# Fixing TensorE's order in the attention of a gated cross-attention and mixture-of-experts block

## The chip, the core and the metric

The kernel runs on one core of a Trainium2 chip. The metric is the device time of one execution in microseconds (us), as the median over several executions. One of them is also taken with the hardware profiler, whose rows the text quotes. PE is TensorE, DVE VectorE, ACT ScalarE, POOL GpSimd, SP SyncE.

## The reference

The input `x` holds 4 x 1024 tokens of 256 values. Each batch entry has 64 context tokens. What is computed, in float32 throughout:

```python
def attention(q, k, v):                       # 16 heads of 64
    qh, kh, vh = q @ w_qs, k @ w_ks, v @ w_vs # per head
    attn = softmax(qh @ kh.T)
    out = (attn @ vh) * qh                    # times the queries
    return concat_heads(out) @ w_proj.T + b_proj

def experts(x):                               # 8 experts, 256 -> 1024 -> 256
    w, sel = top_k(x @ gate_w.T, 2)
    combine = scatter(softmax(w), sel)
    return sum_e(combine[:, e] * (silu(x @ w1[e]) @ w2[e]))

x = x + tanh(g_xattn) * attention(layernorm(x), ctx, ctx)
x = x + tanh(g_ffn) * experts(layernorm(x))
```

## The kernel before

The 4096 tokens are cut into `NG` = 8 groups of 512, and each group into `T` = 4 tiles of 128, which are the steps of the main loop (L1330 to L1378). Two groups belong to one batch entry (`GB` = 2). Sixteen heads are handled as `NP` = 8 pairs. The loop runs over `g` from 0 to 8 and, in it, over `t` from 0 to 3. It is a software pipeline. In step `t` of group `g` stand:

- `probabilities` (L424 to L443): the scores `sc` of the tile in a PSUM pool of two, 16 records on PE, then on DVE the maximum `mx` and the difference `pr`, on ACT the exponential, on DVE the sum `sm` and its reciprocal, and on POOL the product `pr` with the reciprocal.
- `transpose_probabilities` (L454): eight transposes `pa` of the previous step's probabilities, copied by ACT into `aT`. In the program these follow the scores directly.
- `attend` (L469), at step 1 for the previous group: probabilities by values, `po`, in two halves of four head pairs; DVE multiplies each with the queries in `qT` (L478).
- `queries` (L408): the next group's queries, 512 columns for each pair, `pq`, over the steps as `parts` says: four pairs, two, one and one.
- `project` (L486), at steps 2 and 3 for the previous group: `pp`, 32 records of 256 columns for two tiles, which DVE adds to the residual `x` (L493).
- For each pair of groups whose attention is done, the functions `after` and `placing` prepare the experts in eight steps: batch statistics (step 0), the second layernorm's tiles (L312) and their transposes `pt_b` (L317) with the logits `pl` (L508), turned over by a transpose `pl_t` (L518) for the pair's first group (step 1) and the second (step 2), the routing `route` on DVE (step 3), and then `placing` (step 4): the products `prow` (L565, L566) count the tokens ahead of each one. From step 4 on POOL writes the tokens into a table by indirect DMA (L606).
- `ln_norm(g + 2, …)`, at step 2's end: the tiles `xn_a` (L312) of the first layernorm, their transposes `pt_a`, and ACT's copies of them. The tiles live in a pool of three buffers.

`route` compares all logits (L531 to L534), ranks them, and derives `chosen`, a running count `prior`/`taken` of eight pairs of small instructions (L543, L544), and the two weights (L547 to L556). Its `cmp` and `placing`'s `of_choice` share a pool of two buffers with the probabilities `pr`.

The experts run in slots: nine early ones of 256 tokens taken from the first half of the tokens, then wide ones over the rest. A slot's pieces (`ph`, `hT`, `py`) are given out by a generator, `slots`. In groups 6, 7 and the pass after them (`pieces`), some early pieces are handed to the end of a step, as a filling between attention's products; the rest follow after the loop.

What the order of the work comes from: the kernel lists instructions in program order, and a scheduler orders those of each engine by priority and by their estimated costs, unless an instruction is pinned by `pinned(instruction, True)`, which keeps it in program order among the pinned ones. Before the change hardly any of attention's PE instructions is pinned. The scheduler therefore puts `pl` and `pt_a` between scores and moves halves of `po` and products around them. PSUM has a rotating pool of four banks for all products but the scores.

Of the kernel before, what the change touches and what calls it, by code (L numbers as in the profile page):

```python
# [21 lines left out]
def kernel(  # L22
# [254 lines left out]
    def pinned(instruction, pin=True):  # L277
        if pin:
            tc.keep_in_program_order(instruction)

    def ln_stats(groups, name):
        n = len(groups) * T
        mv = small.tile([P, n, 2], F32, tag="mv", name=f"mv_{name}")
        for i in range(n):
            st = small.tile([P, 6], F32, tag="st", name=f"st_{name}_{i}")
            first = nc.vector.bn_stats(st, xg[groups[i // T]][:, i % T, :])
            pinned(first, name == "a0" or i == 0 and name[0] == "a")
            pinned(nc.vector.bn_aggr(mv[:, i, :], st), name == "a0")
        rstd = small.tile([P, n, 1], F32, tag="rstd", name=f"rstd_{name}")
        if name[0] == "a":  # L290
            pinned(nc.scalar.activation(rstd, mv[:, :, 1:2], AF.Sqrt, bias=eps), name == "a0")
            pinned(nc.vector.reciprocal(rstd, rstd), name == "a0")
        else:
            nc.vector.tensor_scalar(rstd, mv[:, :, 1:2], EPS, None, ALU.add)
            nc.gpsimd.tensor_tensor(rstd, rstd, power.unsqueeze(2).to_broadcast([P, n, 1]), ALU.pow)
        return {g: (mv[:, k * T : (k + 1) * T], rstd[:, k * T : (k + 1) * T]) for k, g in enumerate(groups)}

    def ln_norm(g, stats, name):

        mv, rstd = stats[g]  # L300
        nT[g] = npool.tile([P, NC, G], F32, tag="nT", name=f"nT_{name}_{g}")
        first = g == 0 and name == "a"
        keep = None
        if name == "b":
            keep = xg[g]
        elif first:
            keep = npool.tile([P, T, D], F32, tag="nT", name=f"keep_{name}_{g}")
        pt = [bank(f"pt_{name}_{g}_{c}", first) for c in range(NC)]
        for t in range(T):
            xn = keep[:, t, :] if keep is not None else work.tile([P, D], F32, tag="xn", name=f"xn_{name}_{g}_{t}")  # L310
            with behind_sums() if name == "b" else nullcontext():
                scale = nc.vector.tensor_scalar(  # L312
                    xn, xg[g][:, t, :], mv[:, t, 0:1], rstd[:, t, :], ALU.subtract, ALU.mult
                )
            pinned(scale, first)
            for c in range(NC):
                turn = nc.tensor.transpose(  # L317
                    pt[c][:, t * P : (t + 1) * P], xn[:, c * P : (c + 1) * P], ident
                )
                pinned(turn, first)  # L320
        for c in range(NC):
            copy = nc.vector.tensor_copy if first and c else nc.scalar.copy
            pinned(copy(nT[g][:, c, :], pt[c]), first)
# [47 lines left out]
    def values(ctxT):  # L371

        n = 512 // P
        for b0 in range(0, B, 2):
            for p0 in range(0, NP, n):
                pv = bank(f"pv_{b0}_{p0}")
                for c in range(NC):
                    nc.tensor.matmul(
                        pv,
                        ctxT[:, c, b0 * M : (b0 + 2) * M],  # L380
                        wv[:, c, p0 * P : (p0 + n) * P],
                        start=(c == 0),
                        stop=(c == NC - 1),
                    )
                pvv = pv.rearrange("p (q j r k) -> p q j r k", j=2, r=2, k=DK)
                q0 = p0 // 2
                for i in range(2):
                    to = vs[:, b0 + i].rearrange("p (q r) k -> p q r k", r=2)
                    for j in range(2):
                        nc.scalar.copy(  # L390
                            to[j * M : (j + 1) * M, q0 : q0 + n // 2],
                            pvv[i * M : (i + 1) * M, :, j],
                        )
                yield
# [9 lines left out]
    def queries(g, qT, pairs):  # L404
        for p in pairs:
            pq = bank(f"pq_{g}_{p}")
            for c in range(NC):
# [4 lines left out]
                    start=(c == 0),  # L412
                    stop=(c == NC - 1),
                )
                pinned(product, (g, p, c) == (0, 0, 0))
            nc.scalar.copy(of_pair(qT, p), pq)  # L416

    newest = []
# [1 line left out]
    def probabilities(g, t, qT):  # L420

        sc = ps2.tile([P, NP // 2, 2, 2, M], F32, tag="ps2", name=f"sc_{g}_{t}")
        for p in range(NP):
            nc.tensor.matmul(  # L424
                sc[:, p // 2, :, p % 2, :],
                of_pair(qT, p)[:, t * P : (t + 1) * P],
                kT[g // GB][:, p, :],
# [20 lines left out]
    def transpose_probabilities(g, t, pr, aT):  # L448
        prv = pr.rearrange("p (i j) m -> p i (j m)", j=2)
        n = 512 // P  # L450
        for p0 in range(0, NP, n):
            pt = bank(f"pa_{g}_{t}_{p0}")
            for i in range(n):
                nc.tensor.transpose(pt[:, i * P : (i + 1) * P], prv[:, p0 + i, :], ident)  # L454
            nc.scalar.copy(  # L455
                aT[p0 // n][:, :, t * P : (t + 1) * P], pt.rearrange("p (i q) -> p i q", i=n)
            )
# [1 line left out]
    def attend(g, pairs, qT, aT):  # L459

        for q in range(pairs[0] // 2, pairs[-1] // 2 + 1):
# [3 lines left out]
            for r in range(2):  # L465
                for j in range(2):
                    half = slice(j * M, (j + 1) * M)
                    i = q * 2 + r
                    nc.tensor.matmul(  # L469
                        po[j][r * DK : (r + 1) * DK],  # L470
                        vs[half, g // GB, i, :],
                        of_pair(aT, i)[half],
# [7 lines left out]
    def project(g, qT, t0):  # L480

        pp = bank(f"pp_{g}_{t0}").rearrange("p (t d) -> p t d", d=D)
        for i in range(2):
            t = t0 + i
            for p in range(NP):
                nc.tensor.matmul(  # L486
                    pp[:, i, :],
                    of_pair(qT, p)[:, t * P : (t + 1) * P],
                    wp[:, p, :],
# [13 lines left out]
    def logits(g, lg):  # L503

        pl = bank(f"pl_{g}")[:, :P]
        for c in range(NC):
            for t in range(T):
                nc.tensor.matmul(  # L508
                    pl[t * W : (t + 1) * W],
                    gw[:, c, :],  # L510
                    nT[g][:, c, t * P : (t + 1) * P],
# [2 lines left out]
                )  # L514
        lT = work.tile([P, D], F32, tag="xn", name=f"lT_{g}")[:, :P]
        nc.vector.tensor_copy(lT, pl)
        pt = bank(f"pl_t_{g}")[:, :P]
        nc.tensor.transpose(pt, lT, ident)  # L518
        first = g % GB * T
        nc.vector.tensor_copy(  # L520
            lg[:, first : first + T], pt.rearrange("p (t w) -> p t w", w=W)[:, :, :E]
        )

    def route(lg, name):

# [35 lines left out]
    def place(groups, routing, name):  # L561

        rank, weight, chosen, prior = routing
        pr = bank(f"prow_{name}")[:, : R * E]
        nc.tensor.matmul(pr, earlier, chosen.rearrange("p t e -> p (t e)"), start=True, stop=False)  # L565
        nc.tensor.matmul(pr, ones, prior.rearrange("p t e -> p (t e)"), start=False, stop=True)  # L566
        row = scores_of([R, E], f"row_{name}")
        nc.vector.tensor_tensor(
            row,
# [47 lines left out]
    def counts(name):  # L617

        pn = bank(f"pn_{name}")[:, :E]
        nc.tensor.matmul(pn, ones, taken, start=True, stop=True)  # L620
        count = const.tile([1, E], F32, tag=f"count_{name}", name=f"count_{name}")
        nc.vector.tensor_copy(count, pn[0:1, :])
        return count
# [636 lines left out]

    held = {}

    def finish(g, step):

        qT, aT = held[g]
        if step == 1:
            attend(g, range(NP // 2, NP), qT, aT)
        elif step >= 2:
            project(g, qT, (step - 2) * 2)

    def leave(g):
        apart("out", nc.scalar.dma_start(of[g], xg[g]), f"out{g // HG}")

    second = {}
    entered = 0
    done = in_use = None

    def after(g, step):
# [4 lines left out]
            second.update(ln_stats(groups, f"b{g}"))  # L1283
        elif step == 1:
            second["logits"] = scores_of([R, E], f"lg_{g}")
            ln_norm(groups[0], second, "b")
            logits(groups[0], second["logits"])
        elif step == 2:
            for h in groups[1:]:
                ln_norm(h, second, "b")  # L1290
                logits(h, second["logits"])
        elif step == 3:
            second["routing"] = route(second["logits"], f"{g}")
        if step >= 4:
# [8 lines left out]
    def placing(g):  # L1303
# [17 lines left out]
        {1: ([0, 1, 2], [3, 4], [5, 6], [7]), 2: ([], [], [], [0, 1])},  # L1321
        {2: ([2, 3, 4], [5], [6], [7])},
    ]
    parts += [{g + 1: ([0, 1, 2, 3], [4, 5], [6], [7])} for g in range(2, NG - 1)] + [{}, {}]
    value_parts = (2, 1, 1, 0)
    qTs = [halves("qT_0")]
    queries(0, qTs[0], range(NP - 2))
    ln_norm(1, stats, "a")
    queries(0, qTs[0], range(NP - 2, NP))
    for g in range(NG + 1):  # L1330
        attention_ends = g == NG
        if g < NG:
            qT, aT = qTs[g], halves(f"aT_{g}", "hidden" if g % 2 and g + 1 < NG else "group")
            held[g] = (qT, aT)
# [3 lines left out]
        for t in range(T):  # L1338
            if t == 0 and g >= 2:
                leave(g - 2)  # L1340
            if g < NG:
                pr = probabilities(g, t, qT)
            if last:
                transpose_probabilities(*last)

            b = (g - GB - 1) // GB
            ends, behind = b * GB + GB - 1, (g - GB - 1) % GB * T + t if b >= 0 else -1
            if behind == T:
                placing(ends)
            if g and t == 1:  # L1350
                attend(g - 1, range(NP // 2), *held[g - 1])
            for h, pairs in parts[g].items():
                queries(h, qTs[h], pairs[t])
            if 0 <= g - 1 < NG:
                finish(g - 1, t)
            last = (g, t, pr, aT) if g < NG else None
            if g == 0:
                for _ in range(value_parts[t]):
                    next(pending_values)
            if behind >= 0:  # L1360
                after(ends, behind)
            if g == 0 and t == 1:
                tc.keep_in_program_order(nc.scalar.activation(tg, tg, AF.Tanh))
                tc.keep_in_program_order(
# [1 line left out]
                )  # L1366
                for h in range(2):
                    add_bias(h)
            if g + 2 < NG:
                if t == 0 and (g + 2) % GB == 0:  # L1370
                    stats = ln_stats(list(range(g + 2, g + 2 + GB)), f"a{g + 2}")
                elif t == 2:
                    ln_norm(g + 2, stats, "a")
                    add_bias(g + 2)
            if g < 2:
                clear(g * T + t, 2 * T)
            for _ in range(pieces[g][t] if g in pieces else 0):
                next(slots)  # L1378

    leave(NG - 1)  # L1380
    for step in range(2 * T):
        if step == T:
            placing(NG - 1)
        after(NG - 1, step)
        for _ in range((1, 1, 1, 2, 1, 1, 1, 1)[step]):
            next(slots)
    for _ in slots:
# [44 lines left out]
```

## Time and profile before

| | us |
|---|---|
| median of 3 runs | 878.94 (878.19 to 879.98) |
| profiled execution | 880.53 |
| its span | 878.7 |
| PE busy | 842.2 |
| DVE busy | 496.0 |
| ACT busy | 244.6 |
| POOL busy | 265.9 |
| mean granted PE clock (share of full) | 0.987 |

The span is the time from the first to the last instruction of the profiled execution. The busy times of the engines lie beside each other, so they add up to more than the span. A matmul's end in the profile is modelled; two records that run one behind the other are shown overlapping, and the distance between their starts is what PE needs for one.

The first scores of each group start at 65.6 (group 1), 106.6, 150.9, 200.4, 245.6, 295.05 and 340.35 us (group 7); the last projection begins at 435.70, and the first wide slot's products at 539.9.

### The profile page before, as it was taken

What the parts mean: (1) busy time and instruction counts of PE and PEld (TensorE: products, weight loads), DVE (VectorE), ACT (ScalarE), POOL (GpSimd) and SP (SyncE); (2) the same over time, 40 slices, a digit from 0 to 9 for tenths busy, and PEclk for the clock granted to TensorE, in tenths of its full rate; (3) what the DMA queues carried; (4) which work ended last, traced back from release to release, by engine and by line L of the source; (5) the groups of instructions that cost most, each with busy time, mean ns of one, the idle gap of its engine ahead of it and who ended that gap; (6) DMA issues with size and microseconds to landing.
All of it is one profiled execution on the core that took longest, in us unless ns stands there. A gap on an engine that the chain in (4) does not pass through costs nothing.

```text
span 878.7 us, 13306 instructions
## 1 busy us (share of the span) xinstructions
PE 842.2 (96%) x4684; PEld 681.6 (78%) x4684; DVE 496.0 (56%) x1202; ACT 244.6 (28%) x413; POOL 265.9 (30%) x216
## 2 busy tenths in 40 slices
PE   8999999999999999999999699999999999999996
PEld 5555858485767768785888489899999999899995
DVE  4466384679557966862138443665556753546520
ACT  2663242334332323440112012222222221222210
POOL 3052212223721373207224532123222232222132
PEclk9999999999999999999999699999999999999998
DMA  9999999201100055426675668686667675546611
GB/s 197 336 340 341 340 346 340 85 1 60 61 25 1 25 174 163 108 68 189 165 203 147 173 147 215 164 237 140 144 165 178 157 218 133 133 115 176 184 22 37
DMA packets 165032, 141.79 MB, mean 161 GB/s; under 512 B 72685, under 2 KB 159076, under 8 KB 161248
## 3 DMA queue, kind: packets, MB, share of 16 engines
q1 hardware_dynamic: 145456, 118.79, 46.5%
q0 software_dynamic: 12912, 17.11, 10.1%
q10 hardware_dynamic: 6592, 4.98, 1.8%
q8 instruction: 39, 0.64, 0.3%
q14 instruction: 33, 0.27, 0.1%
HBM read 78.73 MB, written 62.46 MB: 161 GB/s over the span
## 4 chain that ended last, share of the span: by engine, by line
PE 77%; DVE 12%; issue 4%; POOL 2%; ACT 2%; DMA 1%; SPq 0%; POOLq 0%; DVEq 0%; ACTq 0%
PE py L1183 20%; PE ph L955 14%; PE ph L1005 11%; PE pp L486 9%; PE pq L408 8%; PE q L1073 5%; PE sc L424 4%; PE pa L454 2%; DVE mx L433 2%; PE po L469 2%; DVE sm L440 1%; DVE pr L435 1%; DVE qT L478 1%; POOL table L606 1%; POOL pr L443 1%
## 5 line engine op out<-in xcount | busy, mean ns | idle before, releaser
L1146 POOL DMA_INDIRECT out_dram<-x,ids x69 | 108.7, 1575 | 306.8 <-DVE x L1161 102.0
L1183 PE MATMUL py<-w,hT 128*128 128x256 f32 (+1 forms) x960 | 186.0, 362 | 0.0
L1183 PEld LDWEIGHTS py<-w,hT 128*128 128x128 f32 (+1 forms) x960 | 160.0, 181 | 21.6 <-issue 1.7
L955 PE MATMUL ph<-xT,w 128*128 128x256 f32 x576 | 135.9, 390 | 7.2 <-issue 7.2
L955 PEld LDWEIGHTS ph<-xT,w 128*128 128x128 f32 x576 | 111.0, 196 | 26.7 <-issue 12.0
L443 POOL TENSOR_TENSOR pr<-pr,sm 128x1024 f32<-128x1024 f32 x32 | 61.4, 1918 | 208.4 <-DVE sm L441 143.0
L408 PE MATMUL pq<-nT_a,wq 128*128 128x512 f32 x256 | 116.1, 597 | 5.7 <-DVE qT L478 3.9
L486 PE MATMUL pp<-wp,qT 128*128 128x256 f32 x512 | 113.5, 379 | 1.3 <-issue 1.3
L486 PEld LDWEIGHTS pp<-wp,qT 128*128 128x128 f32 x512 | 97.0, 190 | 20.0 <-issue 7.4
L408 PEld LDWEIGHTS pq<-nT_a,wq 128*128 128x128 f32 x256 | 46.2, 190 | 58.2 <-issue 44.0
L963 ACT ACTIVATE hT<-ph 128x1024 f32<-128x1024 f32 (+1 forms) x40 | 37.2, 940 | 192.7 <-PE ph L955 119.3
L606 POOL DMA_INDIRECT table<-x,to_row x64 | 62.5, 976 | 42.7 <-DVE x L595 24.8
L424 PEld LDWEIGHTS sc<-keys,qT 128*128 128x128 f32 x512 | 62.6, 192 | 11.2 <-issue 10.8
L424 PE MATMUL sc<-keys,qT 128*128 128x128 f32 x512 | 67.1, 278 | 0.0
L1161 DVE TENSOR_SCALAR x<-py,ids 128x256 f32<-128x256 f32 (+1 forms) x53 | 24.8, 468 | 69.8 <-PE py L1183 63.8
L455 ACT COPY aT<-pa 128x512 f32<-128x512 f32 x64 | 34.7, 592 | 84.1 <-PE pa L454 74.0
L433 DVE TENSOR_REDUCE mx<-sc 128x16 f32<-128x1024 f32 x32 | 39.0, 1219 | 28.0 <-PE sc L424 27.9
L440 DVE TENSOR_REDUCE sm<-pr 128x16 f32<-128x1024 f32 x32 | 39.0, 1219 | 23.9 <-ACT pr L438 21.5
L478 DVE TENSOR_TENSOR qT<-po,qT 128x512 f32<-128x512 f32 x64 | 40.9, 679 | 13.7 <-PE po L469 9.7
L1019 ACT ACTIVATE hT<-hT 128x384 f32<-128x384 f32 (+1 forms) x66 | 33.1, 501 | 51.1 <-DVE hT L1016 48.2
L416 ACT COPY qT<-pq 128x512 f32<-128x512 f32 x64 | 36.5, 581 | 35.3 <-PE pq L408 34.5
L1005 PE MATMUL ph<-x,sa 128*128 128x192 f32 (+1 forms) x264 | 43.6, 314 | 2.0 <-issue 2.0
(278 smaller groups left out, 999.9 us busy)
## 6 DMA issues: line engine op xcount, KB each, us to landing
w<-in_L_ffn_w_dram SPq DMA_DIRECT2D x58, 1024.0 KB
table<-empty SPq DMA_DIRECT2D x8, 5016.0 KB
x<-table SPq DMA_DIRECT2D x116, 64.0 KB
out_dram<-x ACTq DMA_DIRECT2D x8, 512.0 KB
x<-in_x_dram SPq DMA_DIRECT2D x7, 512.0 KB
out_dram<-x,ids POOLq DMA_INDIRECT x69
wq<-in_L_xattn_w_qs_dram SPq DMA_DIRECT2D x4, 256.0 KB
wv<-in_L_xattn_w_vs_dram SPq DMA_DIRECT2D x2, 512.0 KB
```

The source lines that it names most:

```text
L408: product = nc.tensor.matmul(pq, wq[:, c, p * P : (p + 1) * P], nT[g][:, c, :], start=(c == 0), stop=(c == NC - 1),)
L424: nc.tensor.matmul(sc[:, p // 2, :, p % 2, :], of_pair(qT, p)[:, t * P : (t + 1) * P], kT[g // GB][:, p, :], start=True, stop=True,)
L433: nc.vector.tensor_reduce(mx, scv, AX.X, ALU.max)
L440: nc.vector.tensor_reduce(sm, pr, AX.X, ALU.add)
L443: nc.gpsimd.tensor_tensor(pr, pr, sm.unsqueeze(2).to_broadcast([P, H, M]), ALU.mult).ins,
L478: nc.vector.tensor_tensor(own, po[j], own, ALU.mult)
L486: nc.tensor.matmul(pp[:, i, :], of_pair(qT, p)[:, t * P : (t + 1) * P], wp[:, p, :], start=(p == 0), stop=(p == NP - 1),)
L606: nc.gpsimd.indirect_dma_start(out=table.rearrange("r (u w) -> (r u) w", w=2), out_offset=bass.IndirectOffsetOnAxis(ap=to_row[:, k, i : i ...
L955: nc.tensor.matmul(ph[:, i, :], a[:, c, f * P : (f + 1) * P], xT[:, c, :], start=(c == 0), stop=(c == NC - 1),)
L1005: nc.tensor.matmul(to[:, f, :], left[:, (f0 + f) * P : (f0 + f + 1) * P], right, start=not onto and f == 0, stop=True, skip_group_check=on ...
L1146: rows_added = nc.gpsimd.indirect_dma_start(out=outf.rearrange("n (h d) -> (n h) d", d=w)[:rows_of], out_offset=bass.IndirectOffsetOnAxis( ...
L1183: product = nc.tensor.matmul(py[t][i * m : (i + 1) * m], hT[f // per_tile][:, f % per_tile, t * P : t * P + m], b[:, f, i * w : (i + 1) * ...
```

## The change

All PE instructions of attention (scores, transposes, value products, projection, logits, counting products, and for all groups the queries and the first layernorm's transposes) are pinned to program order, and that order is written anew. In a step it is now: at step 1 the first half of `attend`; the scores; the logits `pl` of a group normalised a step before; `prow` if due; the queries; slot pieces in the last two passes; the projection; the transpose `pl_t` of the logits; at step 3 the first layernorm of group `g + 2` (it stood at step 2); the transposes `pa` of the previous step's probabilities; the other parts of `after`; and at step 1 the second half of `attend`. Group 2's queries get the same division over the steps as the others', and the four value products of the start are spread evenly. The logits are a generator now, with its products in a first part and the turning and the copy to `lg` in a second.

```diff
+    steady = False
+    def multiply(*args, **kwargs):
+        pinned(nc.tensor.matmul(*args, **kwargs), steady)
+    def turn(*args):
+        pinned(nc.tensor.transpose(*args), steady)
...
-                pinned(turn, first)
+                pinned(turned, first or steady)
...
-                pinned(product, (g, p, c) == (0, 0, 0))
+                pinned(product, steady or (g, p, c) == (0, 0, 0))
...
         nc.vector.tensor_copy(lT, pl)
+        yield
         pt = bank(f"pl_t_{g}")[:, :P]
-        nc.tensor.transpose(pt, lT, ident)
+        turn(pt, lT, ident)
...
+        yield
...
+    def attend_half(g, half):
+        attend(g, range(half * NP // 2, (half + 1) * NP // 2), *held[g])
...
+    to_route = []
+    def logits_part():
+        for part in to_route:
+            next(part)
...
-            ln_norm(groups[0], second, "b")
-            logits(groups[0], second["logits"])
-        elif step == 2:
-            for h in groups[1:]:
-                ln_norm(h, second, "b")
-                logits(h, second["logits"])
+        if step in (1, 2):
+            ln_norm(groups[step - 1], second, "b")
+            to_route.append(logits(groups[step - 1], second["logits"]))
...
+    parts = [{g + 1: ([0, 1, 2, 3], [4, 5], [6], [7])} for g in range(2)]
...
-    value_parts = (2, 1, 1, 0)
+    value_parts = (1, 1, 1, 1)
...
+        steady = g <= NG
...
+            if g and t == 1:
+                attend_half(g - 1, 0)
             if g < NG:
                 pr = probabilities(g, t, qT)
-            if last:
-                transpose_probabilities(*last)
+            logits_part()
...
-            if g and t == 1:
-                attend(g - 1, range(NP // 2), *held[g - 1])
             for h, pairs in parts[g].items():
-                queries(h, qTs[h], pairs[t])
-            if 0 <= g - 1 < NG:
-                finish(g - 1, t)
-            last = (g, t, pr, aT) if g < NG else None
+                if pairs[t]:
+                    queries(h, qTs[h], pairs[t])
+            for _ in range(pieces[g][t] if g in (NG - 1, NG) else 0):
+                next(slots)
+            if g and t >= 2:
+                project(g - 1, held[g - 1][0], (t - 2) * 2)
...
-            if behind >= 0:
+            logits_part()
+            to_route.clear()
+            if 1 <= behind <= 2 and t == 2:
                 after(ends, behind)
+            if g + 2 < NG and t == 3:
+                ln_norm(g + 2, stats, "a")
+                add_bias(g + 2)
+            if last:
+                transpose_probabilities(*last)
+            last = (g, t, pr, aT) if g < NG else None
+            if behind >= 0 and not (1 <= behind <= 2 and t == 2):
+                after(ends, behind)
+            if g and t == 1:
+                attend_half(g - 1, 1)
...
-            if g + 2 < NG:
-                if t == 0 and (g + 2) % GB == 0:
-                    stats = ln_stats(list(range(g + 2, g + 2 + GB)), f"a{g + 2}")
-                elif t == 2:
-                    ln_norm(g + 2, stats, "a")
-                    add_bias(g + 2)
+            if g + 2 < NG and t == 0 and (g + 2) % GB == 0:
+                stats = ln_stats(list(range(g + 2, g + 2 + GB)), f"a{g + 2}")
...
-            for _ in range(pieces[g][t] if g in pieces else 0):
+            for _ in range(pieces[g][t] if g == HG + 2 else 0):
                 next(slots)
```

After the loop, the two parts of the logits are drawn in the same step.

More of the change, by code (lines that the diff above doesn't have):

```diff
@@ L316, in ln_norm @@
             for c in range(NC):
-                turn = nc.tensor.transpose(
+                turned = nc.tensor.transpose(
                     pt[c][:, t * P : (t + 1) * P], xn[:, c * P : (c + 1) * P], ident
                 )
-                pinned(turn, first)
+                pinned(turned, first or steady)
         for c in range(NC):
@@ L377, in values @@
                 for c in range(NC):
-                    nc.tensor.matmul(
+                    multiply(
                         pv,
@@ L423, in probabilities @@
         for p in range(NP):
-            nc.tensor.matmul(
+            multiply(
                 sc[:, p // 2, :, p % 2, :],
@@ L453, in transpose_probabilities @@
             for i in range(n):
-                nc.tensor.transpose(pt[:, i * P : (i + 1) * P], prv[:, p0 + i, :], ident)
+                turn(pt[:, i * P : (i + 1) * P], prv[:, p0 + i, :], ident)
             nc.scalar.copy(
@@ L468, in attend @@
                     i = q * 2 + r
-                    nc.tensor.matmul(
+                    multiply(
                         po[j][r * DK : (r + 1) * DK],
@@ L485, in project @@
             for p in range(NP):
-                nc.tensor.matmul(
+                multiply(
                     pp[:, i, :],
@@ L507, in logits @@
             for t in range(T):
-                nc.tensor.matmul(
+                multiply(
                     pl[t * W : (t + 1) * W],
@@ L564, in place @@
         pr = bank(f"prow_{name}")[:, : R * E]
-        nc.tensor.matmul(pr, earlier, chosen.rearrange("p t e -> p (t e)"), start=True, stop=False)
-        nc.tensor.matmul(pr, ones, prior.rearrange("p t e -> p (t e)"), start=False, stop=True)
+        multiply(pr, earlier, chosen.rearrange("p t e -> p (t e)"), start=True, stop=False)
+        multiply(pr, ones, prior.rearrange("p t e -> p (t e)"), start=False, stop=True)
         row = scores_of([R, E], f"row_{name}")
@@ L619, in counts @@
         pn = bank(f"pn_{name}")[:, :E]
-        nc.tensor.matmul(pn, ones, taken, start=True, stop=True)
+        multiply(pn, ones, taken, start=True, stop=True)
         count = const.tile([1, E], F32, tag=f"count_{name}", name=f"count_{name}")
@@ L1261 @@
     held = {}
[L1263 to L1269, printed above, removed]
+    def attend_half(g, half):
+        attend(g, range(half * NP // 2, (half + 1) * NP // 2), *held[g])
     def leave(g):
@@ L1384 @@
         after(NG - 1, step)
+        for _ in range(2):
+            logits_part()
+        to_route.clear()
         for _ in range((1, 1, 1, 2, 1, 1, 1, 1)[step]):
```

## The prediction

> **What bounds the kernel now.** I read the page first: its busy shares, its slices and its chain.
>
> ```profile
> span 878.7 us, 13306 instructions
> PE 842.2 (96%) x4684; PEld 681.6 (78%) x4684; DVE 496.0 (56%) x1202; ACT 244.6 (28%) x413; POOL 265.9 (30%) x216
> PE   8999999999999999999999699999999999999996
> PEclk9999999999999999999999699999999999999998
> PE 77%; DVE 12%; issue 4%; POOL 2%; ACT 2%; DMA 1%; SPq 0%; POOLq 0%; DVEq 0%; ACTq 0%
> ```
>
> PE is busy for 842.2 of 878.7 us, at full clock in all slices but one. The change adds and removes no product. So it can gain only PE's gaps, and any wait that it puts on PE lengthens the run directly. What stops PE is in the list of PE's waits:
>
> ```profile
> PE pq L408 <- DVE qT L478: 3.9, 5, 1.4
> PE po L469 <- DVE qT L478: 2.6, 2, 1.7
> PE pa L454 <- POOL pr L443: 2.1, 2, 1.3
> PE pt_b L317 <- DVE qT L478: 2.0, 4, 0.7
> PE prow L566 <- DVE prior L543: 0.7, 1, 0.7
> ```
>
> These are small, but a matmul's modelled end hides part of a wait. I therefore took from the PE timeline the usual distance of two starts without a wait: 0.43 us for a 512-column record (pq), 0.216 for 256 columns (pp: 32 records from 193.50 to 200.40), 0.112 in sc, 0.109 in a transpose. What a stretch takes beyond its records times these is its excess. From 48 to 425 us, where attention runs, the excess is 32.4 us. Some 10 of it is no matter of order: 7.5 falls in 400 to 424, where POOL issues table writes back to back and PE advances at their pace, and 2.6 is scattered. The other 22.2 lies where the change works: first halves of po waiting (0.6 to 1.7 in each of eight groups, about 9), second halves 3, logits put between scores 0.6 in each of six groups, 4, pt_b 2, group 7's po 4. That is the most that a new order can win.
>
> Then I followed the longest dependence that the change touches, from the logits to the routing's product prow. PE first, then DVE:
>
> ```profile
> 189.41 0.27 PE L518 MATMUL pl_t<-ident,lT 128*128 128x128 f32 x1
> 193.50 7.07 PE L486 MATMUL pp<-wp,qT 128*128 128x256 f32 x32
> 200.40 1.95 PE L424 MATMUL sc<-keys,qT 128*128 128x128 f32 x16
> 203.06 0.33 PE L565 MATMUL prow<-chosen,earlier 128*128 128x64 f32 x2
> ```
> ```profile
> 189.72 0.19 DVE L520 COPY lg<-pl_t 128x32 f32<-128x32 f32 x1
> 190.47 1.22 DVE L433 TENSOR_REDUCE mx<-sc 128x16 f32<-128x1024 f32 x1
> 192.93 0.68 DVE L531 TENSOR_TENSOR cmp<-lg 128x512 f32<-128x512 f32 x1
> 194.14 1.22 DVE L440 TENSOR_REDUCE sm<-pr 128x16 f32<-128x1024 f32 x1
> 202.25 0.17 DVE L543 COPY prior<-taken 128x8 f32<-128x8 f32 x1
> 202.54 0.75 DVE L493 SCALAR_TENSOR_TENSOR x<-pp,tg,x 128x512 f32<-128x512 f32 x1
> ```
>
> From the end of the logits' copy (189.91) to the end of the last prior (202.42) DVE needs 12.5 us, softmax work of the same step between. PE has a product pair of queries and 6.9 us of pp to do meanwhile and reaches prow at 203.06, 0.6 after its input: the wait is just covered.
>
> **The change, part by part.** PE now issues its attention products as written. X is the end of the step's projection, S that of its scores.
>
> 1. *prow in groups 4 and 6.* pl_t moves behind the projection; prow stands right after the next group's first scores. Ready: pl_t to the copy's end 0.5 (189.41 to 189.91), plus 12.5: X+13.0. PE until then: pl_t 0.1, the moved transposes pt_a 8 x 0.109 with a wait of 1.05 (part 4), pa 0.87, sc 1.79: X+4.7. The queries, projection and transposes behind prow can't pass it. Stall 8.3, twice: 16.6, against 0.7 before. Bounds: the last routing, with no softmax beside it, took 8.0 from copy (462.31) to prior (470.3), a stall of 3.8; with one more mx and pr (2.45) ahead on DVE 10.8. I take 12.5, as a softmax runs in both steps.
> 2. *prow after the last attention step.* There 8.0 + 0.5, less some 1.6 of expert records that stand ahead of it: 6.9. Bounds 3 and 8.5.
> 3. *pt_b at step 1 (groups 3, 5, 7)* now comes after pa, ahead of po's second half. Its four normalised tiles follow the softmax on DVE: scores' end to the reciprocal's is S+5.3 in the timeline (mx 1.2, pr 1.2, exp on ACT 1.06, sm 1.2, handovers), then
>
> ```profile
> 168.57 2.73 DVE L312 TENSOR_SCALAR x<-x,mv_b,rstd_b 128x256 f32<-128x256 f32 x4
> ```
>
> so S+8.2. PE has two query pairs (2 x 1.72), pa 0.87 and pt_b's own 0.87 for cover, to S+5.2. Some 3.3 twice; in group 7 about 4.8, as the exp there stands behind an activation table load (1.28 at 351.54). 11.4, and 1.3 for the last pair. Bounds 4 and 15: without POOL's product beside it those four tiles take 1.39 (446.57).
> 4. *pt_a at step 3 behind the projection.* Its fourth tile needs a buffer that the first tile's transposes free, and DVE takes x<-pp (0.75) first. PE has 0.75 of work until then; the wait is 0.65 in three groups, 1.05 in two with a routing chain beside, 1.3 in the first: 5.4, against nothing to speak of before. Bounds 2 and 9.
> 5. *po.* The first half follows pa with nothing between, so the wait for ACT's aT copies (0.54 each) less PE's cover is about 0.6 in eight groups, 4.8. Second halves, at the step's end, 0.15 each, 0.9, and twice 2.0 where batch statistics or of_choice on DVE hold the po products back (groups 2 and 4). 9.7, bounds 5 and 15.
> 6. *Group 7, step 0.* The slot pieces are now inside the step; ACT has the exp until S+3.9, then a table load 1.28, hT 1.09, a load 1.28 and the aT copies 1.08 (rows 346.10 to 351.54), with handovers of 0.8: S+9.4. PE is there at S+4.3: 5.1, bounds 2 and 7.
>
> The even spread of value products, of the second group's query pairs and the later statistics only reorder work before 100 us, where PE has products queued: nothing, at most 2 if that cover fails. DMAs: the late table's entries follow the same routing. It lies 5.6 us earlier against the last projection and 6.9 us of expert products move ahead of that, so the first wide slot stays covered.
>
> Sum: 16.6 + 6.9 + 11.4 + 1.3 + 5.4 + 9.7 + 5.1 = 56.4 of new excess in place of 22.2: +34.2.
>
> 7. *Clock.* PE's clock drops after PE has stood still, in this trace:
>
> ```profile
> 404.00:408.00 4.00, 1.91 (x8) 0.39 (x8) 1.38 (x2) 0.00 (x0) 3.09 (x4) 0.99 1.14 303
> 408.00:411.00 3.00, 3.00 (x11) 1.56 (x6) 0.69 (x1) 0.00 (x0) 2.39 (x3) 0.50 0.80 164
> 490.00:495.00 5.00, 1.76 (x3) 0.86 (x3) 0.93 (x6) 0.00 (x0) 3.78 (x5) 0.50 0.54 210
> 500.00:502.00 2.00, 2.00 (x6) 1.61 (x5) 1.98 (x14) 0.00 (x0) 1.40 (x1) 0.50 0.95 288
> ```
>
> (Columns: stretch, length, busy time of PE, PEld, DVE, ACT, POOL, granted clock, DMA share, GB/s.) Work resumed at 0.50; 21 records near 498 took 7.45 us instead of 4.54, so a drop costs up to 2.9. I charge the two stalls of 8.3: 5.8, between none and five (also the three of about 5), 14.5. "TensorE: Matmul & The Clock Gate" of the Trainium skill, Part 1, says that the gate halves the clock after one idle window of about 3.4 us and opens after about as long of work; the half clock from 407.9 to 411.3 agrees. Speaking against this change, it would put all five stalls at half clock, an estimate of 1.7 each, 8.5 together, and the time at 921.5.
>
> 34.2 + 5.8 = 40.0 on the profiled execution, 878.7 of span and 880.5 with what lies around it. That is 1.6 over the median of the runs, so 878.9 + 40.0 = 918.9.
>
> **The rivals.**
>
> *The stalls are much shorter: 896.* With DVE's scheduler putting routing ahead of softmax, the chain is the 8.0 of the last routing, and 2 x 4.5 goes; x_b at 1.39 takes off 1.3 three times, part 5's two special waits (4.0) vanish, and no clock drops (5.8): 9.0 + 3.9 + 4.0 + 5.8 = 22.7 less, 896. For it: the softmax result isn't due for a while. Against: its reduce comes ahead by the rows above. Chance 0.24.
>
> *Faster: 877 or less.* The one mechanism is that DVE has the routing ready by X+4.7 and the normalised tiles by S+5.2; then only 56.4 less parts 1 to 3 (36.2), 20.2, stands against 22.2 before: 2 gained, 877, and 12 gained, 867, should half of the 20.2 be covered too. It decides from a chain under 4.7, where rows show 8.0 at best. Chance 0.06, and 0.02 for a draw within 0.2%, about what a measurement of this kernel can tell from no change.
>
> *More follows: 937.* The late routing delays the table's writes so that the first wide slot (539.9) waits for its tokens. About 97 us of expert work lies between it and the last projection, so the cover is wide, but the POOL bursts that cost 12.2 at 480 to 498 could hit another stage. 919 + 12 and, with a second one, + 24: 931 to 943. Chance 0.08. The forecast keeps 0.60.
>
> **How the numbers follow.** The forecast's own range is 905 to 932 (parts 1 to 6 with half of their bounds, clock 0 to 14.5). Taking in the half stalls leaves out about 0.1 on either side (the faster cases below, most of the last rival above): 892 to 934. Slower by over 0.2% has 0.60 + 0.24 + 0.08 = 0.92.
>
> **What would show it.** The waits of PE should list prow <- DVE prior near 24 us in three places, and pt_b <- DVE x near 12; PE's busy share falls to about 92%, with clock slices below 9 near 200, 300 and 440. Wrong would be a prow without a wait: then pl_t's lateness was covered, and the rest of the sum is small.

## The result and the profile after

The changed kernel takes 933.16 us (median of 6 runs, 931.06 to 935.64) against 878.96 for the kernel before measured beside it: a ratio of 1.0618, 95% interval 1.0600 to 1.0637, 54.2 us slower. Its profiled execution, 935.64 us, is the longest of the six and has a span of 933.9. The kernel before took 863 us in some sets of runs and 879 to 881 in others, with the changed kernel moving along, so the experiments below are given as ratios to the kernel before measured beside each.

The head of the changed kernel's page, in the order of the lines shown of before (without the chain, which here is a single write at the end):

```profile
span 933.9 us, 13325 instructions
PE 857.9 (92%) x4684; PEld 688.4 (74%) x4684; DVE 503.0 (54%) x1202; ACT 248.8 (27%) x417; POOL 265.5 (28%) x216
PE   8999999896998689688989979999999999999996
PEclk9999999897999979899899979999999999999998
```

The same 4684 products now fill 92% of a longer span. PE's row drops to 6 or 8 in nine of the slices from the eighth to the twenty-first (the 7 in the twenty-fourth has its like in before's 6), and the clock's row to 7 or 8 in five of them or beside them. PE's longest waits in the changed kernel, without those that the profile gives no releaser for:

```profile
PE prow L285 <- DVE prior L555: 13.0, 3, 6.3
PE pt_b L327 <- DVE x L322: 7.9, 6, 1.5
PE ph L967 <- DVE xT L940: 7.6, 2, 4.0
PE prow L285 <- DVE chosen L552: 7.3, 2, 3.6
PE po L285 <- ACT aT L465: 5.7, 7, 3.9
PE py L1195 <- DVE qT L488: 5.2, 1, 5.2
PE pt_a L327 <- DVE xn_a L322: 4.2, 6, 1.2
```

prow waits 20.3 us in all, where 0.7 stood before. New besides: pt_b at 7.9, pt_a, and ph, the first expert products, which wait for their tokens. The 5.2 of py, at 465 to 470 us, falls where POOL writes the table back to back; the like stretch of the kernel before, between 400 and 424, had 7.5 us beyond its records.

By the starts of a group's first scores (the profiled executions, before and after) the difference is 6.3 us at group 4 (200.40 and 206.69), 20.3 at group 5, 22.8 at group 6 and 34.5 at group 7 (340.35 and 374.88). At the 32 ph records that follow all attention work (486.24 and 542.18) it is 55.9, and the rest of the run is the same. Groups 4 and 6 take 14.0 and 11.8 of it; these are the two with a prow. The largest share, 21.4, arises in group 7 and the pass after it.

The stretch around the first prow, from the timeline of the changed kernel:

```profile
203.79 0.27 PE L289 MATMUL pl_t<-ident,lT 128*128 128x128 f32 x1
203.99 0.75 DVE L503 SCALAR_TENSOR_TENSOR x<-pp,tg,x 128x512 f32<-128x512 f32 x1 [3.83 <-PE pp L285]
204.66 0.18 DVE L531 COPY lg<-pl_t 128x32 f32<-128x32 f32 x1
205.81 1.04 PE L289 MATMUL pa<-ident,pr 128*128 128x128 f32 x8
206.96 1.15 DVE L543 TENSOR_TENSOR cmp<-lg 128x512 f32<-128x512 f32 x1 [1.34 <-PE pa L289]
212.27 0.41 PE L285 MATMUL prow<-chosen,earlier 128*128 128x64 f32 x2 [3.64 <-DVE chosen L552]
216.24 1.84 DVE L555 COPY prior<-taken 128x8 f32<-128x8 f32 x1
218.94 0.69 PE L285 MATMUL prow<-prior,ones 128*128 128x64 f32 x2 [6.26 <-DVE prior L555]
219.42 9.47 PE L418 MATMUL pq<-nT_a,wq 128*128 128x512 f32 x16
229.87 0.22 DVE L590 SCALAR_TENSOR_TENSOR of_choice<-rank,row 128x64 f32<-128x64 f32 x1 [9.90 <-PE pa L289]
```

The logits' copy ends at 204.84, one microsecond after the projection, as DVE takes the projection's result (x, 0.75) first. But the first compare, cmp, begins only at 206.96, and the column in brackets says that DVE idled 1.34 us before it for PE's pa. The scores end near 208.5 and prow's second part starts at 218.94: 10.4 us, in which PE has only the two records of prow's first part. Then the sixteen records of queries take 9.3 us instead of 6.9. The last row is a second wait of the same kind: of_choice, which takes a buffer of the same pool as cmp, waits 9.90 us for pa, which now stands behind the queries. The table's writes follow from it.

### The profile page after: what moved, and what is told of

Read it like the earlier page. It is cut to its first block, busy times and chain, and to the rows that moved or that the text cites. A ratio compares the mean times of both kernels' runs of the same rounds, so it can differ in the third digit from the quotient of the medians.

```text
span 933.9 us, 13325 instructions
## 1 busy us (share of the span) xinstructions
PE 857.9 (92%) x4684; PEld 688.4 (74%) x4684; DVE 503.0 (54%) x1202; ACT 248.8 (27%) x417; POOL 265.5 (28%) x216
## 5 line engine op out<-in xcount | busy, mean ns | idle before, releaser
L1195 PE MATMUL py<-w,hT 128*128 128x256 f32 (+1 forms) x960 | 190.7, 367 | 5.2 <-DVE qT L488 5.2
L1195 PEld LDWEIGHTS py<-w,hT 128*128 128x128 f32 (+1 forms) x960 | 162.7, 184 | 28.6 <-DVE qT L488 6.1
L418 PE MATMUL pq<-nT_a,wq 128*128 128x512 f32 x256 | 121.2, 618 | 1.3 <-DVE qT L488 1.2
L418 PEld LDWEIGHTS pq<-nT_a,wq 128*128 128x128 f32 x256 | 48.3, 199 | 52.4 <-issue 48.3
L285 PEld LDWEIGHTS sc<-keys,qT 128*128 128x128 f32 x512 | 60.5, 194 | 13.9 <-issue 13.9
L285 PE MATMUL sc<-keys,qT 128*128 128x128 f32 x512 | 64.5, 280 | 0.0
```

Of the source, the lines that this page charges most:

```text
L285: pinned(nc.tensor.matmul(*args, **kwargs), steady)
L418: product = nc.tensor.matmul(pq, wq[:, c, p * P : (p + 1) * P], nT[g][:, c, :], start=(c == 0), stop=(c == NC - 1),)
L1195: product = nc.tensor.matmul(py[t][i * m : (i + 1) * m], hT[f // per_tile][:, f % per_tile, t * P : t * P + m], b[:, f, i * w : (i + 1) * ...
```

## The experiments

Each result is a ratio to the kernel before, with its 95% interval. One per cent is 8.8 us at 879, and the differences in us below are worked out with it.

**The changed kernel again.**

> The changed kernel itself once more, beside the kernel before, as the measure for the runs that undo one part of it: the kernel before took 863 here and 879 in its first runs, so ratios and not differences are to be compared. If the change costs the same work in both, 1.062 of before; if part of its cost hung on what made the first runs longer (the stretch in which POOL's table writes hold up the other engines, 11 to 12 us in both first profiles), the ratio stays near 1.06 and that stretch is shorter in both.

1.0616 (1.0598 to 1.0634), with the kernel before at 863.25. The ratio holds. The stretch of table writes at the end of the early slots (from 486 us in the kernel before, from 542 in the changed one) cost 11.4 us over its records in the first profile of the changed kernel and is gone in this one, so it has no part in the difference. What makes it was not tried.

**prow later in its step.**

```diff
-            if behind == T:
-                placing(ends)
             for h, pairs in parts[g].items():
...
             last = (g, t, pr, aT) if g < NG else None
+            if behind == T:
+                placing(ends)
```

> The changed kernel with prow and what hangs on it placed behind the queries and the turned probabilities of its step (groups 4, 6 and the pass after 7) instead of right after the scores. Theory A (prow's place on PE makes the stall): the routing is ready some 15 us after the projection's end by the changed kernel's trace, PE now has 12.4 us of work until then, so the wait at prow falls from 10.4 to about 3 in each of the two groups, and the half clock behind it (2.4 and 3.0 us) goes: some 20 us less, about 913. Theory B (the routing, not prow's place, sets the pace; the table and its readers come when routing ends): group 4 gains its 8 to 10, but in group 6 PE only meets the wait later, at the first expert slot, where ph waits 4.0 us for its tokens now: the tokens' wait grows by about 8, and the gain is about 10, 923.

1.0348 (1.0323 to 1.0373): 23 us of the 54 go with this move alone. PE's waits of this run:

```profile
PE prow L285 <- DVE prior L555: 5.5, 3, 2.4
PE ph L967 <- DVE xT L940: 4.2, 1, 4.2
```

prow's waits fall from 20.3 to 5.5 and the one for tokens in group 7 stays at 4.2. Theory A holds: the products queued behind prow were what paid. The wait for tokens that theory B saw growing did not grow.

**The turned logits ahead of the projection.**

```diff
+            logits_part()
+            to_route.clear()
             if g and t >= 2:
                 project(g - 1, held[g - 1][0], (t - 2) * 2)
...
-            logits_part()
-            to_route.clear()
             if 1 <= behind <= 2 and t == 2:
```

> The changed kernel with pl_t (the turned logits) ahead of the projection again, as in the kernel before, and prow left where the change put it. Theory A (the stall is the routing's length less PE's work between pl_t and prow): the routing starts 6.9 us earlier, the waits at prow fall from 10.4 to about 3.5 in groups 4 and 6, the half clock behind them goes, and the table is written 7 us earlier, so the wait for tokens in group 7 (4.0) goes too: 14 + 5 + 4 = 23 less, about 910. Theory B (other work on DVE, the softmax, takes the 7 us): waits at prow fall by under 3 each, time above 922.

1.0575 (1.0538 to 1.0612), a gain of under 4 us where theory A promised 23. The timeline of this run says why:

```profile
198.11 0.27 PE L289 MATMUL pl_t<-ident,lT 128*128 128x128 f32 x1
198.42 0.19 DVE L531 COPY lg<-pl_t 128x32 f32<-128x32 f32 x1
206.73 1.04 PE L289 MATMUL pa<-ident,pr 128*128 128x128 f32 x8
207.88 1.15 DVE L543 TENSOR_TENSOR cmp<-lg 128x512 f32<-128x512 f32 x1 [1.47 <-PE pa L289]
219.87 0.69 PE L285 MATMUL prow<-prior,ones 128*128 128x64 f32 x2 [6.01 <-DVE prior L555]
```

The logits lie ready from 198.61 on, and cmp still begins at 207.88, right after pa. cmp takes one of two buffers that hold probabilities; the older of these is free only when its probabilities have been turned. The change moved pa from behind the scores to the end of the step, and this is the second thing that holds routing back.

**A buffer for cmp, without and with the early logits.**

```diff
-        cmp = soft.tile([P, 2, R, E, E], F32, tag="pr", name=f"cmp_{name}")
+        cmp = small.tile([P, 2, R, E, E], mybir.dt.uint8, tag="cmp", bufs=1, name=f"cmp_{name}")
```

> The changed kernel with the routing's cmp in a buffer of its own (as 8 bit integers, since the memory is full; its values are 0 and 1) instead of one of the two that hold probabilities. Theory C (formed after the turned logits came early for nothing): routing begins when the turning of the step's probabilities frees cmp's buffer, 2.9 us after the projection, and not when the logits are there, 1.05 after it. Then routing starts 1.9 earlier in groups 4 and 6: 2 to 4 us less in all. Theory A (the logits alone set it): the same within 1.

> Both together: cmp in its own buffer and pl_t ahead of the projection. Theory C: routing can begin 7 us before the projection ends; by the changed kernel's trace it needs about 12 us from the logits' copy, so prow's input is there at most 1 to 3 us after PE reaches prow, in place of 10.4: 15 to 18 less in two groups, 5 less of half clock, 4 less of waiting for tokens in group 7: 22 to 27 less than the changed kernel, about 1.03 of before. If a third thing holds routing (softmax first on DVE), under 8 less.

The buffer alone gives 1.0619 (1.0601 to 1.0637), nothing, as theory A of that run had it: cmp begins at 206.78, half a microsecond after the logits' copy, and one of its four operations then takes 2.36 us beside a POOL addition (x plus bias, 206.95 to 209.93) instead of 0.68, which eats the little that was won. With the logits early as well it is 1.0322 (1.0303 to 1.0340), 26 us less. Each of the two alone is worth nothing or under 4 us, since the other still stands in the way. From the timeline of the run with both:

```profile
196.23 0.69 DVE L543 TENSOR_TENSOR cmp<-lg 128x512 uint8<-128x512 f32 x1
207.78 0.33 PE L285 MATMUL prow<-chosen,earlier 128*128 128x64 f32 x2
208.38 0.43 PE L285 MATMUL prow<-prior,ones 128*128 128x64 f32 x2 [0.26 <-DVE prior L555]
```

Routing now runs beside the projection, and prow follows the scores with a wait of 0.26. One part of the forecast didn't come: of the two waits for tokens the one in the pass after is gone, but the one in group 7 stays, 4.3 us. There of_choice still waits for pa (3.02 us, at 216.72).

**Extra work in the wait.**

```diff
+            if behind == T and g < NG:
+                busy = bank(f"busy_{g}")
+                for _ in range(11):
+                    pinned(nc.tensor.matmul(busy, ident, wq[:, 0, :512], start=True, stop=True))
             if behind == T:
                 placing(ends)
```

> The changed kernel with eleven products of 512 columns, whose result nobody reads, put between the scores and prow in groups 4 and 6: 22 records of 0.43, 9.45 us of PE work where PE stands still for 10.4 now. They add work and take away no wait. Theory (what follows the stall, the queries at half clock, is a cost of standing still): the queries behind prow take 6.9 instead of 9.3 and 9.9, so the kernel gets 5.4 us faster by extra work, 1.055 of before instead of 1.0616. Rival (the queries are slow for another reason, as DVE or ACT being behind): no change, or up to 2 us slower.

1.0580 (1.0548 to 1.0613). The whole time alone doesn't decide, as the interval reaches the changed kernel's. The rows do. Timeline of this run:

```profile
208.54 9.61 PE L1366 MATMUL busy<-wq,ident 128*128 128x512 f32 x22
219.02 0.43 PE L285 MATMUL prow<-prior,ones 128*128 128x64 f32 x2 [0.71 <-DVE prior L555]
219.30 7.08 PE L418 MATMUL pq<-nT_a,wq 128*128 128x512 f32 x16
```

prow's second part comes when it came in the changed kernel, at 219, and the queries behind it take 7.08 instead of 9.47, though nothing changed but that PE had something to do. Windows over the queries' start, in the changed kernel and then in this run (the column after POOL's is the granted clock):

```profile
220.00:224.00 4.00, 4.00 (x6) 1.55 (x5) 0.00 (x0) 0.59 (x1) 0.00 (x0) 0.50 0.00 0
```
```profile
220.00:224.00 4.00, 4.00 (x10) 1.71 (x9) 0.00 (x0) 1.17 (x2) 0.00 (x0) 1.00 0.00 0
```

So 2.4 us in group 4, and 3.0 by the same rows in group 6, are the price of the clock.

**po ahead of the second layernorm.**

```diff
+            if g and t == 1:
+                attend_half(g - 1, 1)
             if behind >= 0 and not (1 <= behind <= 2 and t == 2):
                 after(ends, behind)
-            if g and t == 1:
-                attend_half(g - 1, 1)
```

> The changed kernel with the second half of po ahead of the transposes pt_b at step 1 (groups 3, 5, 7 and the pass after). Theory A (pt_b waits for its tiles because nothing lies between): pt_b's waits, 2.5, 2.0 and 2.5 us beyond its records, fall under 0.7 each, and the slow po and sc records behind it (1.8 and 0.6 in group 3) go with them: 8 to 11 us less, 922 to 925. Rival (DVE is the limit: the po products wait behind the four tiles and the scores' maximum comes later): no more than 3 less, 930 or above.

1.0605 (1.0576 to 1.0634): the rival is right. The wait has another name, and is nearly as long:

```profile
PE pt_b L327 <- DVE qT L488: 6.8, 6, 2.5
```

DVE still has softmax, four tiles and now the po products to do before the short step ends.

**The second layernorm a step later.**

```diff
-            if 1 <= behind <= 2 and t == 2:
-                after(ends, behind)
+            if behind == 2:
+                after(ends, 1)
+                after(ends, 2)
...
-            if behind >= 0 and not (1 <= behind <= 2 and t == 2):
+            if behind >= 0 and behind not in (1, 2):
```

> The changed kernel with the second layernorm's transposes pt_b of both groups behind the projection of step 2 and both groups' logits in step 3. Moving po ahead of pt_b only turned its wait for the tiles into a wait for DVE's po products. Theory A' (pt_b at step 1 is at fault, as whatever stands ahead of it there, DVE has softmax, po products and the four tiles to do in one short step): at step 2 the projection's 6.9 us cover DVE. In groups 3, 5 and 7 step 1 loses 6.4, 3.5 and 6.5 to 7.5 us now beyond its records (waits before and in pt_b 4.0, 3.5 and 5.0, the rest po and scores at half clock behind them), in the waits for tiles and the slow records behind them: 13 to 17 less, 1.042 to 1.047. Rival (DVE's backlog goes on and stops po's second half or the queries there): under 5 less, 1.056 or above.

1.0434 (1.0411 to 1.0457), 16 us less, as theory A' had it. Behind the projection the sixteen transposes are nearly free of waits, and po and scores run at full clock again in group 3:

```profile
170.67 2.02 PE L285 MATMUL po<-aT,vs 64*64 64x512 f32 x16
172.63 2.05 PE L285 MATMUL sc<-keys,qT 128*128 128x128 f32 x16
184.77 0.98 PE L327 MATMUL pt_b<-ident,x 128*128 128x128 f32 x7 [0.49 <-DVE x L503]
```

**The expert pieces at the step's end.** The loop that draws `pieces` in the last two passes goes back behind everything else.

> The changed kernel with the expert pieces of the last two passes at the end of their steps again, all else as changed. Theory A (the pieces wait on PE for their tokens, 4.0 us in group 7 and 3.6 in the pass after, because they come too early in the step): these two waits, the half clock behind the first and most of po's wait for aT in group 7 (3.9) go: 10 to 14 less, 919 to 923. Rival (the pieces were good cover; without them pa or po wait instead for the softmax and the copies, which nothing covers now): within 4 of 933, or slower.

1.0547 (1.0529 to 1.0564), 6 us, between the two. Of the waits for tokens only the 3.6 in the pass after is gone. In group 7 the first ph still waits 3.20 (listed without a releaser; DVE turned the tokens just before), and its sixteen records still take 5.3 us for 3.5. po's wait for aT falls from 5.7 to 1.7, but 3.9 come back at pt_b, which has no cover now in group 7:

```profile
379.96 5.38 PE L967 MATMUL ph<-xT,w 128*128 128x256 f32 x16 [3.20 <-issue]
395.82 0.66 PE L327 MATMUL pt_b<-ident,x 128*128 128x128 f32 x2 [4.97 <-DVE x L322]
```
```profile
PE pt_b L327 <- DVE x L322: 11.8, 6, 5.0
PE po L285 <- ACT aT L465: 1.7, 6, 0.3
```

**The same program order, unpinned.**

```diff
-        steady = g <= NG
+        steady = False
```

> The changed kernel's program order with no attention product pinned, so that the scheduler orders PE again. Theory A (fixing the order is what costs, since the scheduler would put ready work ahead of prow and pt_b): prow's and pt_b's waits nearly vanish and the time comes within 1.5% of before. Rival (the new program order itself, late probabilities and logits, makes the dependences late; the scheduler can't mend it): over 3% above before.

1.0445 (1.0418 to 1.0472): the rival's case, over 3% above before, though not all of the cost. The scheduler takes 15 of the 54 us back and pt_b's wait shrinks to 3.3, but prow still waits 12.4 in all. Another order of PE's work did not bring late inputs forward here.

**What was found, put together, and unpinned.** cmp's buffer, the early logits, the second layernorm a step later, the pieces at the step's end, and the first layernorm's transposes behind pa; then the same without pins.

> The changed kernel with all that the runs named mended, the fixed order kept: cmp in its own buffer, pl_t ahead of the projection, pt_b and logits a step later, the expert pieces at the step's end, and the first layernorm's transposes behind the turned probabilities. If the parts add up (25 us from routing, 6 from the pieces, 13 to 17 from pt_b, 4 to 6 from pt_a, less 2 that they share), 48 to 52 of the 54 go: 1.002 to 1.006 of before, and any fixed order's own cost is nil. If fixing the order costs by itself, or waits come back elsewhere: 1.015 or above. Below 1.0 it would beat both kernels.

> The kernel with the waits cut (1.012 of before), with no attention product pinned. It tells what fixing the order costs by itself, once no dependence is late. Theory (a fixed order can't step round a wait, however small: 8.6 us at pt_a and some 10 in group 7 and the pass after are left, and a scheduler lets ready products go ahead of them): 5 to 12 us less, 0.998 to 1.006 of before; under 1.0 it would beat both kernels. Rival (what is left has nothing else ready to put ahead, or the scheduler's own gaps are as large): 1.009 to 1.016.

Pinned, it is 1.0120 (1.0101 to 1.0139): 44 of the 54 us are accounted for by these edits. The single gains of the parts with a run of their own, 26, 16 and 6, make 48, so they overlap by 4 or more, as pt_a's move, which has no run of its own, is in it too. Among the waits left are small ones:

```profile
PE pt_a L327 <- DVE x L503: 3.5, 2, 1.8
PE pt_a L327 <- DVE xn_a L322: 2.3, 3, 1.6
PE prow L285 <- DVE prior L555: 1.5, 3, 0.7
```

Unpinned it is 1.0049 (1.0030 to 1.0069): 6 us more, inside what the theory said of the fixed order, and still a little slower than the kernel before. None of the versions beats it. In both the first ph of group 7 still waits, 3.4 and 3.5 us, for its tokens.

## Why the prediction was right, and where its steps were not

The forecast, slower with 918.9 and up to 934, holds at 933.2, within 1 us of its upper end. The mechanism is right: late dependences stop a PE whose order is fixed. That the size still fits is in part luck, as two terms that were too large (parts 2 and 5, by 10.6) made up for others that were too small. The term sums were made on PE's excess, and so is the comparison, from the changed kernel's trace. The excess from 40 us to the end went from 50.9 to 106.3. In the new places it is 72 us where the sum had 62; of before's own, 34 us are left, 17 gone where the sum had 22.

- *Part 1, prow in groups 4 and 6*: 10.6 each, 21.2 instead of 16.6. The place and the queue behind it were right, as the move of prow shows (23 us with its clock). The chain was mis-sized by 2.1 us. The copy of the logits ended at X+1.05 and not X+0.5, as DVE took the projection's result first (part 4 counted this, part 1 did not), and from there to the last prior (204.84 to 218.89) it took 14.05 us instead of 12.5, of which 1.34 is the idle time before cmp; the softmax work in it is the same as before. The stated cause was half of it: the chain was said to start from pl_t's move. It is held twice, by pl_t and by pa's move to the step's end, through cmp's buffer; the runs with one and with both undone show this.
- *Part 2, prow after the last step*: 6.9 forecast, 0.4 found. The routing took the 8 us expected, but PE was itself held 3.6 us by the wait for tokens ahead of it and then ran py at half clock. The stall was there, under another name; the forecast had no wait for tokens in it.
- *Part 3, pt_b*: 4.0, 3.5 and 5.0, 12.5 beside 11.4. Right, by the step-later run too, though the sum's own marks, S+8.2 and S+5.2, are 3.0 apart and not the 3.3 that it took twice.
- *Part 4, pt_a*: 5.7 beside 5.4. No run of its own.
- *Part 5, po*: 2.7 in first halves and about 3 in groups 2 and 4, 5.6 instead of 9.7. The mis-sized terms: PE's wait for aT, 0.45 in six groups and not 0.6 in eight; the special waits, 1.4 and 1.5 and not 2.0 each; and the 0.9 of second halves, which hardly shows.
- *Part 6, group 7*: 8.3 instead of 5.1. The wait for aT is there (4.1), but 4.2 is a wait of ph for tokens, which the forecast put at nothing, as it looked only at the first wide slot's tokens. They come later: the first ph ran at 343.01 in the kernel before, 2.7 us after the group's first scores, without a wait, and at 380.84 in the changed one, 6.0 after them (rows below).
- *Part 7, the clock*: 5.4 behind the two prows, as charged (5.8). But it also dropped behind pt_b and in group 7 and the pass after, about 9.5 more by records at half pace (po 3.62 for 1.81 in group 3), 15 in all. This is the upper end of the bound, 14.5, and it makes most of the 14 us between forecast and result.

The first ph of group 7 in the kernel before, and then two rows of the changed kernel:

```profile
343.01 3.62 PE L955 MATMUL ph<-xT,w 128*128 128x256 f32 x16
```
```profile
341.98 0.23 DVE L590 SCALAR_TENSOR_TENSOR of_choice<-rank,row 128x64 f32<-128x64 f32 x1 [10.50 <-PE pa L289]
380.84 5.41 PE L967 MATMUL ph<-xT,w 128*128 128x256 f32 x16 [4.02 <-DVE xT L940]
```

In group 6 of_choice, and with it the table, waits 10.50 us for pa. This fits the wait of group 7's first ph, which is 3.2 to 4.3 us in the profile of every version here but the kernel before, also where prow no longer waits. No run put pa back behind the scores, so this cause is argued and not shown.

Of the signs it named, the busy share of 92% and the clock's dips near 220, 340 and 455 us came; prow's wait is 20.3 in two places and not 24 in three, and pt_b's is 7.9 after DVE's x, with 2.3 more put down to ACT. Of the rivals, the shorter stalls had nothing for them: DVE takes softmax work between the routing's steps, as the rows of before had shown. The first wide slot did not wait. The estimate from the Trainium skill's "TensorE: Matmul & The Clock Gate", half clock after five stalls, put the clock's cost at 8.5, nearer to the 15 found than the 5.8 for two stalls that the sum took (with it the sum gives 921.6, where the prediction has 921.5).

## What to carry to other kernels

Before an order is fixed by hand, list for each product not only what it reads but which buffer its producers wait for: here a transpose moved to the end of a step held a two-buffer pool, and through it a chain on another engine. In a fixed order a late product stops everything that is queued behind it, and the longer stops were paid a second time in clock here; put long chains beside the long product runs. Where two things hold a chain, undoing one shows little (0 and under 4 us here, 26 for both), so undo both before the theory is dropped.

## What the runs showed of the hardware

PE's clock drops without a single long gap. In group 3 of the changed kernel no wait of PE at pt_b is above 1.5 us, yet, in windows of 2 us:

```profile
170.00:172.00 2.00, 0.70 (x7) 0.49 (x6) 1.97 (x4) 1.41 (x3) 0.33 (x1) 1.00 0.00 0
172.00:174.00 2.00, 0.52 (x3) 0.29 (x3) 2.00 (x3) 0.00 (x0) 1.57 (x1) 0.76 0.00 0
174.00:176.00 2.00, 2.00 (x10) 1.19 (x13) 0.37 (x2) 0.86 (x2) 0.00 (x0) 0.50 0.00 0
```

PE was busy for 1.2 of the 4 us from 170 on. By the clock's column it dropped to half at about 173 and stayed there to about 179.8 (0.50 in 176 to 178, 0.54 in 178 to 180). "TensorE: Matmul & The Clock Gate" of the Trainium skill, Part 1, speaks of an idle window of some 3.4 us as the trigger; here a window that was mostly idle was enough.

A DVE copy of 128x8 values took 1.84 us instead of 0.17 (216.24 in the changed kernel) while POOL's product of the probabilities ran (1.90 from 216.15 on). "SBUF — State Buffer" of the Trainium skill, "SBUF: two separate sides", says that the two engines share a port pair that one holds for a whole instruction; the row agrees.
